# Adding p to eight row blocks by accumulating transfers, in a fused block-attention and residual LayerNorm kernel

## The chip, the cores and the metric

One core of a Trainium2 chip. The metric is the device time of one execution in microseconds; a kernel's time is the median of its runs, and one more execution is recorded by the hardware profiler.

## The reference

x has 8 batches of 512 x 1024 floats. Each batch is cut into 8 blocks of 64 rows; a block's rows are summed, the sums are projected by Wk, scored against one query vector and weighed by a softmax; their weighted sum is projected by Wo. The result, one vector p per batch, is added to every row, and a LayerNorm of that is added to x. Cut to what matters:

```python
block_repr = x.reshape(B, 8, 64, H).sum(axis=2)
keys = rms_norm(block_repr @ Wk.T) * rms_weight
attn = softmax((keys * query[1]).sum(-1))
p = ((attn[..., None] * block_repr).sum(1) @ Wo.T)[:, None, :]
z = x + p
out = x + (z - z.mean(-1)) / sqrt(z.var(-1) + 1e-6) * gamma + beta
```

## The kernel before

The 4096 rows are worked on as 32 row blocks ("rows" below) of 128 partitions x 1024 floats. Two of them make a tile of 1 MB, loaded and stored as one. Batches go in three groups of 2, 4 and 2: the first has rows 0 to 7 (tiles x0.0 to x0.3), the second rows 8 to 23 (x1.0 to x1.7), the third rows 24 to 31. Rows are gathered in units: 0 and 1 (first group), 2 to 5 of four rows each (8-11, 12-15, 16-19, 20-23), then 6 (24-27), 7 and 8 (two rows each).

For each group: `bs` (TensorE) sums the blocks of each tile as it lands; `col` (VectorE) transposes the sums; `proj.0` multiplies by Wk; `sm` is a softmax of small steps that go between VectorE, ScalarE, GpSimd and TensorE; `proj.1` multiplies by Wo; `v` weighs (vw), `p mm` spreads p over the partitions and two copies `p cp0` and `p cp1` bring its halves to SBUF (pb); `tb` writes p's rows into a small table for TensorE, by transfers.

For each row k of a group, with p there:

- `S` (VectorE, line 646) x <- x + p, with its sum over the row in tot.
- `Q` (ScalarE, line 648) squares of (sum - 1024 x), summed: the variance.
- per unit, the small steps `U.. v` (variance with epsilon), `std`, `rs` (its inverse), `s2` and `sd2` (entries of a stats matrix), mostly on GpSimd; `U.. mm` transposes that matrix on TensorE and `U.. lt` copies it to SBUF.
- `D` (VectorE, line 746) (gamma + std) * x into a pair of PSUM banks; `R` (TensorE, line 732) adds mean, beta and p as products of the stats matrix and the table; `E` (ScalarE, line 761) scales by rs and writes the result over x; `st` stores a tile (SP's queue).

Every engine works its queue in order. The queues are written out by hand in ORDER, a list of step numbers in which a word such as `72:7` gives a tile's slot (of 13) or a PSUM bank, a letter picks one of a step's engines, and `f`, `h`, `z` words are TensorE's products with zeros, which set a bank's state or fill time. The PSUM pairs 0, 2 and 4 hold the rows between D and E; a D waits until the E of the row that held its pair before is done. Loads, `tb` and stores are all issued by SP; a load into a slot that held another tile waits for that one's last reader or its store.

The kinds of a unit are set by UKIND. In the kernel before all are 'c', the path above; two other kinds are in the code and not in use.

Of the kernel before, what the change touches and what calls it, by code (L numbers as in the profile page):

```python
# [10 lines left out]
ALU = mybir.AluOpType  # L11
# [7 lines left out]
GROUPS = (2, 4, 2)  # L19
XSLOTS = 13  # L20
UNITS = ((4, 4), (4, 4, 4, 4), (4, 2, 2))
# [3 lines left out]
NTAB = 2  # L25
UKIND = 'ccccccccc'
TABS = ((0, 'y'), (1, 'y'), (2, 'y'))
# [15 lines left out]
ORDER = (  # L43
# [21 lines left out]
)  # L65
# [65 lines left out]
def block_attn_resid_kernel(  # L131
# [55 lines left out]
    def bank(name):  # L187
        return bank_at(plan.at[name])
# [25 lines left out]
    blkT = [alloc(f"blkT{i}", [P, HC, 32]) for i in range(2)]  # L214
    vw = [alloc(f"vw{i}", [P, QU]) for i in range(2)]
    pb = [alloc(f"pb{i}", [P, H]) for i in range(2)]
# [307 lines left out]
    def spread_out(G):  # L524

        n, g = G["n"], G["g"]
        name = f"proj{n}.1"
        w = vw[n % 2]
        add(f"v{n} w", [(ACT, 0.47), (DVE, 0.42)], lambda e: nc.scalar.activation(
            w, bank(name)[:, :QU], AF.Identity, scale=wcol) if e == ACT else nc.vector.tensor_scalar(  # L530
            w, bank(name)[:, :QU], wcol, None, ALU.mult), reads=["wcol"], writes=[f"vw{n % 2}"], use=name, release=name)
        part = f"p{n}"

        add(f"{part} mm", [(PE, 1.0)], lambda e: spread_p(G, part, True), reads=[f"vw{n % 2}", f"spread{g}"], claim=("P", part))
        for i in range(2):
            add(f"{part} cp{i}", [(ACT, 0.6), (DVE, 0.69)], lambda e, i=i: copy(
                e, bands(pb[n % 2])[:, :, i, :], half(part, i).rearrange("p (q d) -> p q d", d=P)),
                reads=[("slot", part)], writes=[f"pb{n % 2}.{i}"], release=part)

    def spread_p(G, part, start):  # L540
        n, g = G["n"], G["g"]
        for j in range(2):
            for i in range(2):
                lo = slice(64 * i, 64 * i + 64)
                nc.tensor.matmul(
                    half(part, i).rearrange("p (q j d) -> p j q d", j=2, d=HB)[:, j], spread[g][lo, j, :],
                    vw[n % 2][lo, :].rearrange("p (q d) -> p q d", d=HB),
                    start=start and j == 0, stop=True, tile_position=(64 * i, 0), skip_group_check=True,
                )
# [26 lines left out]
    def form_of(k):  # L576

        return "y" if kind_of(k) == "c" else "x"

# [10 lines left out]
    def before(k):  # L590

        q, r = unit_of[k]
        u = q % NU
        if kind_of(k) == "b":
            b = ubn[:, k % 2]
            add(f"B{k}", [(DVE, 1.24)], lambda e: both_halves(b, x_row(k)), reads=[xk(k)], writes=[f"ubn{k % 2}"])
            add(f"C{k}", [(DVE, 0.2)], lambda e: nc.vector.bn_aggr(out=umv[u][:, r, :], in_=b),
                reads=[f"ubn{k % 2}"], writes=[f"umv{u}.{r}"])
        elif kind_of(k) == "p":
            add(f"B{k}", [(ACT, 1.28)], lambda e: nc.scalar.activation(square, x_row(k), AF.Identity, accum_out=usx[u][:, r : r + 1]),  # L600
                reads=[xk(k)], writes=[f"usx{u}.{r}"])

    def before_p(G):
# [14 lines left out]
    def moments(k):  # L618
# [14 lines left out]
        elif kind == "p":  # L633
            y = f"y{k}"

            def go():
# [3 lines left out]
                spread_p(G, y, False)  # L640
            add(f"Y{k}", [(PE, 2.75)], lambda e: go(), reads=["ident", xk(k), f"vw{n}", f"spread{g}"], claim=("t", y))
            add(f"Q{k}", [(ACT, 1.28)], lambda e: nc.scalar.activation(
                square, flat(pair(y)), AF.Square, bias=total, scale=-float(H), accum_out=ssq),
                reads=[S], writes=[Q], use=y, release=[y, y])
        else:
            add(f"S{k}", [(DVE, 1.15)], lambda e: nc.vector.scalar_tensor_tensor(  # L646
# [4 lines left out]
    def totals(q):  # L651
# [7 lines left out]
        t = pmv[n]  # L659
        if UKIND[q] == "p":  # L660
            add(f"U{q} to", [(POOL, 0.5)], lambda e: nc.gpsimd.tensor_scalar(
# [6 lines left out]
    def unit(q):  # L668
# [5 lines left out]
        T = f"U{q}"  # L674
        st, lt = stat[i][:, :U], lts[i]
        S4 = [f"tot{i}.{r}" for r in range(U)]
# [6 lines left out]
        if UKIND[q] == "b":  # L683
# [4 lines left out]
                reads=Q4, writes=[V])  # L688
            add(f"{T} v", [(E, c)], lambda e: engine[e].tensor_tensor(v, v, a, ALU.add), reads=[f"ua{u}"], writes=[V])
        else:  # L690
            add(f"{T} v", [(E, c), (ACT, 0.25)] + ([(DVE, 0.18)] if slow else []), lambda e: nc.scalar.activation(  # L691
# [5 lines left out]
        else:  # L697
            inverse_root(T, v, r0, a, rs, (V, f"u0{u}", f"ua{u}", f"urs{u}"))
            add(f"{T} sd", [(E, c)], lambda e: engine[e].tensor_tensor(std, v, rs, ALU.mult), reads=[V, f"urs{u}"], writes=[S])
        add(f"{T} s2", [(E, c)], lambda e: engine[e].tensor_scalar(  # L700
            st[:, :, :, 0], tot[i][:, :U].unsqueeze(2).to_broadcast([P, U, 2]), -UP / H, None, ALU.mult),
            reads=S4, writes=[f"stat{i}.s"])
        D, own = f"stat{i}.d", f"stat{i}.n"
        W = 1 + MAXG if UKIND[q] == "c" else 1
        if W == 1 and (q < NST or UKIND[q - NST] == "c" or units[q - NST][0] < G["first"]):
            add(f"{T} sn", [(POOL, c + 0.1)], lambda e: nc.gpsimd.tensor_scalar(
# [197 lines left out]
```

## Time and profile before

| | us |
|---|---|
| median of three runs | 147.21 (146.16 to 147.56) |
| profiled execution | 145.84 |
| its span (first to last instruction) | 144.1 |
| VectorE busy | 98.1 (68%) |
| ScalarE busy | 89.4 (62%) |
| TensorE busy with products | 113.1 (79%) |
| GpSimd busy | 54.3 (38%) |

Busy times are from the profiled execution. A busy TensorE is not one at its peak, since its products overlap and some only fill time. Instructions that overlap by their start and end on one engine (S lasts 1.22 us, and the next begins 1.15 us after it) are counted once in a stretch's busy time.

### The profile page before, as it was taken

Reading aid. Unit: us, or ns where it says so; the run is one execution under the profiler, and the core shown is the slowest. Engines: PE = TensorE matmul, PEld = TensorE weight load, DVE = VectorE, ACT = ScalarE, POOL = GpSimd, SP = SyncE. Lnnn points to the kernel's source line nnn. Section 1 sums busy time; section 2 is a strip of 40 time slices with the busy share of each in tenths; the row PEclk is TensorE's granted clock in tenths of the full one; section 3 lists DMA queues with packets and bytes.
Section 4 is the critical chain, followed back from the end, with each engine's and each line's share of the span. In section 5 each row is a group of like instructions: output and inputs, shape, how many; then the busy total and the mean of one; then the engine's idle time right before and its main releaser. Section 6 shows DMA issues by size and latency. Waiting matters only on the chain.

```text
span 144.1 us, 2877 instructions
## 1 busy us (share of the span) xinstructions
PE 113.1 (79%) x1096; PEld 57.9 (40%) x1104; DVE 98.1 (68%) x163; ACT 89.4 (62%) x137; POOL 54.3 (38%) x108
## 2 busy tenths in 40 slices
PE   5987754989999676999673969979698798369660
PEld 2556452848985322543321224434254222123210
DVE  2056330315215996667989999999998999997920
ACT  3020210113931998065689999799979999989640
POOL 6888800000000073038001876138348009994000
PEclk9999998699999999999999599999779968999955
DMA  4999999999999997006399867644653651837894
GB/s 127 429 412 421 416 401 420 408 409 425 412 430 418 417 413 324 18 2 289 130 332 416 332 262 296 255 180 184 259 218 161 266 232 73 357 155 291 326 367 184
DMA packets 7526, 42.76 MB, mean 297 GB/s; under 512 B 808, under 2 KB 808, under 8 KB 3672
## 3 DMA queue, kind: packets, MB, share of 16 engines
q1 hardware_dynamic: 7440, 42.54, 73.0%
q8 instruction: 8, 0.13, 0.4%
q10 hardware_dynamic: 72, 0.04, 0.1%
q14 instruction: 6, 0.05, 0.1%
HBM read 25.73 MB, written 16.78 MB: 295 GB/s over the span
## 4 chain that ended last, share of the span: by engine, by line
DMA 28%; DVE 22%; PE 19%; ACT 11%; POOL 10%; issue 6%; POOLq 1%; DVEq 0%
DVE x L646 10%; DVE t L746 9%; DMA gam<-in_L_cond_ln_gamma_dram 9%; DMA x<-in_L_cond_Wo_dram 8%; PE b L473 7%; DMA x<-in_L_cond_Wk_dram 6%; POOL ustd L695 4%; ACT x L761 4%; PE t L407 4%; ACT square L648 3%; POOL urs L715 3%; DMA tab<-in_L_cond_ln_gamma_dram 3%; PE t L732 3%; DMA pb<-in_cond_dram 3%; ACT woT L241 2%
## 5 line engine op out<-in xcount | busy, mean ns | idle before, releaser
L746 DVE SCALAR_TENSOR_TENSOR t<-gam,ustd,x 128x1024 f32<-128x1024 f32 x31 | 39.0, 1290 | 5.7 <-ACT x L761 2.7
L648 ACT ACTIVATE square<-x,tot 128x1024 bf16<-128x1024 f32 x32 | 36.7, 1147 | 2.9 <-DVE x L646 2.0
L761 ACT ACTIVATE x<-t,urs 128x1024 f32<-128x1024 f32 x31 | 33.3, 1105 | 7.3 <-PE t L732 5.4
L646 DVE SCALAR_TENSOR_TENSOR x<-x,pb 128x1024 f32<-128x1024 f32 x32 | 37.4, 1216 | 0.1
L732 PE MATMUL t<-tab,lt 32*128 32x512 f32 x124 | 23.4, 652 | 3.3 <-DVE lt L243 2.1
L869 PE MATMUL b<-zeros 128*128 128x512 bf16 (+1 forms) x69 | 21.7, 452 | 3.0 <-DVE zeros L294 1.6
L407 PE MATMUL t<-ident,x 128*128 128x128 f32 x120 | 16.7, 300 | 4.3 <-DMA x<-in_L_cond_Wk_dram 2.7
L700 POOL TENSOR_SCALAR stat<-tot 128x8 f32<-128x8 f32 (+1 forms) x8 | 5.7, 714 | 36.6 <-DVE x L646 36.6
L407 PEld LDWEIGHTS t<-ident,x 128*128 128x128 f32 x120 | 15.8, 199 | 5.5 <-issue 4.8
L869 PEld LDWEIGHTS <-zeros 128*128 128x128 bf16 x90 | 9.5, 116 | 20.2 <-issue 15.9
L715 POOL TENSOR_TENSOR urs<-uv,halfs 128x4 f32<-128x4 f32 (+1 forms) x8 | 12.8, 1604 | 8.5 <-DVE uv L692 8.2
L429 PE MATMUL b<-x,blk 128*32 128x256 f32 x128 | 9.4, 416 | 5.9 <-DMA x<-in_x_dram 5.0
L241 ACT COPY wkT<-t 128x1024 f32<-128x1024 f32 x3 | 3.0, 1012 | 16.8 <-PE t L407 16.8
L732 PEld LDWEIGHTS t<-tab,lt 32*128 32x128 f32 x124 | 6.8, 186 | 14.3 <-issue 5.3
L243 DVE COPY wkT<-t 128x1024 f32<-128x1024 f32 x5 | 6.0, 1221 | 9.5 <-PE t L407 9.5
L695 POOL TENSOR_TENSOR ustd<-uv,halfs 128x4 f32<-128x4 f32 (+1 forms) x8 | 11.1, 1387 | 1.1 <-ACT uv L691 0.9
L473 PE MATMUL b<-wkT,blkT 128*32 128x256 f32 x192 | 11.0, 381 | 0.6 <-DVE blkT L439 0.6
L429 PE MATMUL t<-x,blk 128*32 128x256 f32 x128 | 8.1, 383 | 2.7 <-DMA x<-in_x_dram 2.7
L241 ACT COPY woT<-t 128x1024 f32<-128x1024 f32 x5 | 4.9, 1008 | 7.7 <-PE t L407 7.7
L486 POOL TENSOR_TENSOR ca<-c 128x8 f32<-128x8 f32 x3 | 1.6, 530 | 19.9 <-ACT c L485 19.9
L473 PE MATMUL b<-woT,blkT 128*32 128x256 f32 x128 | 7.9, 383 | 0.9 <-DVE lt L243 0.9
L473 PEld LDWEIGHTS b<-wkT,blkT 128*32 128x32 f32 x192 | 5.9, 110 | 5.8 <-DVE blkT L439 1.8
(93 smaller groups left out, 106.4 us busy)
## 6 DMA issues: line engine op xcount, KB each, us to landing
x<-in_x_dram SPq DMA_DIRECT2D x16, 1024.0 KB
out_dram<-x SPq DMA_DIRECT2D x14, 1024.0 KB
x<-in_L_cond_Wk_dram SPq DMA_DIRECT2D x4, 1024.0 KB
x<-in_L_cond_Wo_dram SPq DMA_DIRECT2D x3, 1024.0 KB
out_dram<-x SPq DMA_DIRECT2D x3, 512.0 KB
x<-in_L_cond_Wo_dram SPq DMA_DIRECT2D x2, 512.0 KB
gam<-in_L_cond_ln_gamma_dram SPq DMA_DIRECT2D x1, 512.0 KB
out_dram<-x SPq DMA_DIRECT2D x2, 256.0 KB
```

Source lines behind the costliest of these rows:

```text
L241: nc.scalar.copy(dst, src)
L407: nc.tensor.transpose(half(part, c // 4)[:, bass.ts(c % 4, P)], tile_of(name)[:, e % RT, c::HC], ident)
L429: nc.tensor.matmul(bank(f"bs{n}")[32 * j : 32 * j + 32, :QU], blk[G["g"]], tile_of(name)[:, r, bass.ts(j, QU)], start=(t == 0 and r == 0), ...
L473: nc.tensor.matmul(bank(name)[32 * j : 32 * j + 32, :QU], b[:, c, :], w[:, c, j], start=(c == 0), stop=(c == HC - 1),)
L646: add(f"S{k}", [(DVE, 1.15)], lambda e: nc.vector.scalar_tensor_tensor(x_row(k), x_row(k), 1.0, pb[n], ALU.mult, ALU.add, accum_out=total) ...
L648: add(f"Q{k}", [(ACT, 1.28)], lambda e: nc.scalar.activation(square, x_row(k), AF.Square, bias=total, scale=-float(H), accum_out=ssq), rea ...
L695: add(f"{T} std", [(POOL, 0.5 + 0.16 * U)], lambda e: nc.gpsimd.tensor_tensor(std, v, halfs[:, :1].to_broadcast([P, U]), ALU.pow), reads=[ ...
L715: add(f"{T} rs", [(POOL, 0.5 + 0.16 * U)], lambda e: nc.gpsimd.tensor_tensor(rs, v, halfs[:, 1:].to_broadcast([P, U]), ALU.pow), reads=[V, ...
L732: nc.tensor.matmul(half(f"row{k}", h), lts[q % NST][lo : lo + 32, r // RT, :], tab_of(k)[0][lo : lo + 32, :], start=False, stop=True, skip ...
L746: add(f"D{k}", [(DVE, 1.21)], lambda e: nc.vector.scalar_tensor_tensor(flat(pair(name)), gam, std, x_row(k), ALU.add, ALU.mult), reads=["g ...
L761: add(f"E{k}", [(ACT, 1.13)], lambda e: nc.scalar.activation(x_row(k), flat(pair(name)), AF.Identity, scale=rs), reads=[RS], writes=[xk(k) ...
L869: nc.tensor.matmul(bank_at(i)[:, :n], zeros, zeros[:, 0:1].to_broadcast([P, n]), start=start, stop=True, skip_group_check=True)
```

## The change

Unit 3 (rows 12 to 15) becomes kind 'a' and unit 4 (rows 16 to 19) kind 'd'. For both, S is gone; four transfers `A12`, `A14`, `A16`, `A18`, issued by GpSimd, each add pb to a tile of two rows in SBUF (read x, read p, write x).

- 'a': a step B per row sums x before p is added (`tensor_reduce` on VectorE for rows 12, 13 and 15, ScalarE for row 14); `Bp1.0` sums p (VectorE); `U3 to` (GpSimd) adds the two; Q follows as before, on the row with p.
- 'd': B is two `bn_stats` over half a row each, C is `bn_aggr`, both VectorE, on the row with p; U4's v and s2 are made from them, and there is no Q.

The slots of x go from 13 to 14, and vw from two buffers to one. ORDER is new throughout. The core of the diff:

```diff
-XSLOTS = 13
+XSLOTS = 14
-UKIND = 'ccccccccc'
+UKIND = 'cccadcccc'
...
+ADD_ISSUE = 1.3
+ADD_MB = 2.0
...
-    vw = [alloc(f"vw{i}", [P, QU]) for i in range(2)]
+    vw = [alloc("vw0", [P, QU])]
...
+        elif kind_of(k) in "pa":
+            sx = usx[u][:, r : r + 1]
+            add(f"B{k}", [(ACT, 1.34), (DVE, 1.2)], lambda e: nc.scalar.activation(
+                square, x_row(k), AF.Identity, accum_out=sx) if e == ACT else nc.vector.tensor_reduce(sx, x_row(k), AX.X, ALU.add),
                 reads=[xk(k)], writes=[f"usx{u}.{r}"])
...
+        if mine & set("bpa"):
+            add(f"Bp{n}.0", [(ACT, 1.34), (DVE, 1.2)], lambda e: nc.scalar.activation(
+                square, pb[n % 2], AF.Identity, accum_out=t[:, 0:1]) if e == ACT else nc.vector.tensor_reduce(
+                t[:, 0:1], pb[n % 2], AX.X, ALU.add),
...
+        elif kind in "ad":
+            if place[k][1] % RT == 0:
+                tile_ = x_name(k)
+                add(f"A{k}", [(POOL, ADD_ISSUE)], lambda e: nc.gpsimd.dma_start(
+                    out=tile_of(tile_), in_=pb[n].unsqueeze(1).to_broadcast([P, RT, H]), accum_op=ALU.add),
+                    reads=p_keys, writes=[xk(k), xk(k + 1)], mb=ADD_MB)
+            if kind == "a":
+                add(f"Q{k}", [(ACT, 1.34)], lambda e: nc.scalar.activation(
+                    square, x_row(k), AF.Square, bias=total, scale=-float(H), accum_out=ssq), reads=[xk(k), S], writes=[Q])
+            else:
+                b = ubn[:, k % 2]
+                add(f"B{k}", [(DVE, 1.3)], lambda e: both_halves(b, x_row(k)), reads=[xk(k)], writes=[f"ubn{k % 2}"])
+                add(f"C{k}", [(DVE, 0.2)], lambda e: nc.vector.bn_aggr(out=umv[u][:, r, :], in_=b),
+                    reads=[f"ubn{k % 2}"], writes=[f"umv{u}.{r}"])
...
+        elif UKIND[q] == "d":
+            add(f"{T} v", [(E, c), (DVE, 0.18)] if slow else [(E, c)], lambda e: engine[e].tensor_scalar(
+                v, umv[u][:, :U, 1], UP * UP, EPS * UP * UP, ALU.mult, ALU.add),
```

The queues of the second group that ORDER gives, before and after, from gamma's scaling to the third group's S24 (small softmax steps left out):

```
VectorE before: gam up, col1, D0, D1, U0 lt, D2, U1 v, sm1.., D3, sm1.., D4, sm1.., D5, U1 lt, sm1.., D6, D7, S8 to S16,
  D8, D9, D10, col2, S17, S18, D11, D12, S19, U3 lt, sm2.., D13, D14, S20, S21, D15, S22, sm2.., S23, U4 lt, D16, D17,
  sm2.., D18, sm2.., v2, D19, D20, S24
VectorE after: col1, gam up, D0, D1, D2, sm1.., D3, sm1.., D4, sm1.., D5, U1 lt, sm1.., p1 cp0, S8, S9, D6, S10, S11, D7,
  Bp1.0, D8, D9, S20, S21, D10, D11, S22, col2, S23, D12, D13, D14, B17, sm2.., B16, C16, C17, B19, C19, D15, sm2..,
  B18, C18, sm2.., U4 v, U5 lt, sm2.., v2, D16, D17, D18, S24
ScalarE before: E4, p1 cp1, p1 cp0, E5, Q8 to Q14, E6, E7, U2 lt, Q15, Q16, E8, E9, Q18, sm2.., E10, E11, Q19, Q17, E12, E13
ScalarE after: p1 cp1, E4, Q8, Q9, E5, Q10, Q11, U2 v, E6, E7, Q12, U2 lt, Q13, E8, E9, Q14, Q15, U3 v, Q22, E10, E11, Q23,
  sm2.., U3 lt, Q21, Q20, U5 v, E12, E13
GpSimd after: U1's steps, sm1.., A12, A14, A16, A18, U2 s2, U2 std, U3 to, U2 sd2, U3 s2, U2 rs, U3 std, U3 rs, U3 sd2, U5's, U4's
SP after: tb0, x2.1, st1, st3, x2.2, tb1, x2.3, st5, st7, st9, st11, st13, st15, tb2, st17
```

Ahead of this, B12, B13 and B15 stand on VectorE around the first group's v0 (B12, B13, v0, B15, p0 cp0, S0) and B14 on ScalarE ahead of p0 cp1. Two of TensorE's fills stand between the parts of the second group's first projection, ahead of D2. The second group's third pair of PSUM banks is given up: bank 0 holds the third group's block sums (`bs2`) from before p1 until col2, and rows 6 to 11 use pairs 2 and 4. On SP, x2.1 is loaded ahead of st1, x2.2 after st3, x2.3 after the second group's `tb`.

## Rows read from the trace of the kernel before

**Rows 1.** The page: busy us of each engine, share of the span, instructions.
```profile
PE 113.1 (79%) x1096; PEld 57.9 (40%) x1104; DVE 98.1 (68%) x163; ACT 89.4 (62%) x137; POOL 54.3 (38%) x108
```

**Rows 2.** Busy time by stage: from:to, length, busy us (instructions), clock, transfers' share, GB/s.
```profile
40.00:57.00 17.00, 13.90 (x257) 7.48 (x251) 11.33 (x20) 11.17 (x19) 3.86 (x5) 1.00 0.99 408
57.00:74.00 17.00, 14.53 (x177) 6.56 (x182) 12.46 (x24) 8.71 (x17) 4.38 (x4) 1.00 0.36 132
74.00:90.00 16.00, 12.17 (x124) 4.57 (x121) 16.00 (x25) 15.27 (x24) 8.59 (x9) 0.89 0.83 332
90.00:110.00 20.00, 17.45 (x168) 8.21 (x161) 19.20 (x34) 18.03 (x29) 9.45 (x14) 0.91 0.51 211
110.00:132.00 22.00, 17.29 (x74) 6.03 (x74) 21.08 (x29) 20.60 (x32) 12.18 (x11) 0.92 0.55 228
```

**Rows 3.** TensorE's timeline (start, us, what, idle before): block sums as tiles land.
```profile
49.87 1.07 PE L429 MATMUL t<-x,blk 128*32 128x256 f32 x16 [1.39 <-DMA x<-in_x_dram]
...
52.36 1.07 PE L429 MATMUL t<-x,blk 128*32 128x256 f32 x16 [0.66 <-DMA x<-in_x_dram]
...
54.85 1.07 PE L429 MATMUL t<-x,blk 128*32 128x256 f32 x16 [0.67 <-DMA x<-in_x_dram]
```

**Rows 4.** The chain that ended last (start, us, what): two transfers, and the tail.
```profile
39.20 4.45 DMA tab<-in_L_cond_ln_gamma_dram
...
43.67 12.40 DMA gam<-in_L_cond_ln_gamma_dram
...
132.23 1.25 POOLq L899
...
133.50 0.17 DVE ua L487
```

**Rows 5.** VectorE's timeline.
```profile
42.86 0.48 DVE L530 TENSOR_SCALAR vw<-t,wcol 128x256 f32<-128x256 f32 x1 [3.54 <-PE t L459]
...
45.60 1.23 DVE L646 SCALAR_TENSOR_TENSOR x<-x,pb 128x1024 f32<-128x1024 f32 x1
...
56.10 0.69 DVE L352 TENSOR_SCALAR gam<-gam 128x1024 f32<-128x1024 f32 x1 [1.25 <-DMA gam<-in_L_cond_ln_gamma_dram]
...
75.05 1.22 DVE L646 SCALAR_TENSOR_TENSOR x<-x,pb 128x1024 f32<-128x1024 f32 x1
...
76.20 1.22 DVE L646 SCALAR_TENSOR_TENSOR x<-x,pb 128x1024 f32<-128x1024 f32 x1
...
84.22 3.68 DVE L746 SCALAR_TENSOR_TENSOR t<-gam,ustd,x 128x1024 f32<-128x1024 f32 x3
87.81 0.44 DVE L439 STREAM_TRANSPOSE blkT<-b 128x256 f32<-128x256 f32 x1
...
111.56 1.22 DVE L646 SCALAR_TENSOR_TENSOR x<-x,pb 128x1024 f32<-128x1024 f32 x1
```

**Rows 6.** ScalarE's timeline.
```profile
44.79 0.59 ACT L241 COPY pb<-b 128x512 f32<-128x512 f32 x1 [4.05 <-PE b L545]
...
75.17 1.15 ACT L648 ACTIVATE square<-x,tot 128x1024 bf16<-128x1024 f32 x1 [0.50 <-DVE x L646]
...
76.44 1.15 ACT L648 ACTIVATE square<-x,tot 128x1024 bf16<-128x1024 f32 x1
...
88.63 2.10 ACT L761 ACTIVATE x<-t,urs 128x1024 f32<-128x1024 f32 x2
```

**Rows 7.** VectorE's copies in the list of groups: busy us, mean ns.
```profile
L243 DVE COPY lt<-b 128x256 f32<-128x256 f32 x3 | 1.3, 417 | 0.0
...
L243 DVE COPY pb<-b 128x512 f32<-128x512 f32 x1 | 0.7, 692 | 1.5 <-PE b L545 1.5
```

**Rows 8.** GpSimd's timeline.
```profile
54.94 0.25 POOL L700 TENSOR_SCALAR stat<-tot 128x8 f32<-128x8 f32 x1
...
78.73 1.08 POOL L700 TENSOR_SCALAR stat<-tot 128x8 f32<-128x8 f32 x1 [10.85 <-DVE x L646]
...
80.99 1.91 POOL L715 TENSOR_TENSOR urs<-uv,halfs 128x4 f32<-128x4 f32 x1
```

More of the change, by code (lines that the diff above doesn't have):

```diff
@@ L527, in spread_out @@
         name = f"proj{n}.1"
-        w = vw[n % 2]
+        w = vw[0]
         add(f"v{n} w", [(ACT, 0.47), (DVE, 0.42)], lambda e: nc.scalar.activation(
             w, bank(name)[:, :QU], AF.Identity, scale=wcol) if e == ACT else nc.vector.tensor_scalar(
-            w, bank(name)[:, :QU], wcol, None, ALU.mult), reads=["wcol"], writes=[f"vw{n % 2}"], use=name, release=name)
+            w, bank(name)[:, :QU], wcol, None, ALU.mult), reads=["wcol"], writes=["vw0"], use=name, release=name)
         part = f"p{n}"
-        add(f"{part} mm", [(PE, 1.0)], lambda e: spread_p(G, part, True), reads=[f"vw{n % 2}", f"spread{g}"], claim=("P", part))
+        add(f"{part} mm", [(PE, 1.0)], lambda e: spread_p(G, part, True), reads=["vw0", f"spread{g}"], claim=("P", part))
         for i in range(2):
@@ L546, in spread_p @@
                     half(part, i).rearrange("p (q j d) -> p j q d", j=2, d=HB)[:, j], spread[g][lo, j, :],
-                    vw[n % 2][lo, :].rearrange("p (q d) -> p q d", d=HB),
+                    vw[0][lo, :].rearrange("p (q d) -> p q d", d=HB),
                     start=start and j == 0, stop=True, tile_position=(64 * i, 0), skip_group_check=True,
@@ L576, in form_of @@
     def form_of(k):
-        return "y" if kind_of(k) == "c" else "x"
+        return "y" if kind_of(k) in "cad" else "x"
     def tab_of(k):
@@ L598, in before @@
                 reads=[f"ubn{k % 2}"], writes=[f"umv{u}.{r}"])
-        elif kind_of(k) == "p":
-            add(f"B{k}", [(ACT, 1.28)], lambda e: nc.scalar.activation(square, x_row(k), AF.Identity, accum_out=usx[u][:, r : r + 1]),
+        elif kind_of(k) in "pa":
+            sx = usx[u][:, r : r + 1]
+            add(f"B{k}", [(ACT, 1.34), (DVE, 1.2)], lambda e: nc.scalar.activation(
+                square, x_row(k), AF.Identity, accum_out=sx) if e == ACT else nc.vector.tensor_reduce(sx, x_row(k), AX.X, ALU.add),
                 reads=[xk(k)], writes=[f"usx{u}.{r}"])
@@ L607, in before_p @@
         mine = {UKIND[q] for q, (first, _) in enumerate(units) if G["first"] <= first < G["first"] + G["rows"]}
-        if mine & set("bp"):
-            add(f"Bp{n}.0", [(ACT, 1.28)], lambda e: nc.scalar.activation(square, pb[n % 2], AF.Identity, accum_out=t[:, 0:1]),
+        if mine & set("bpa"):
+            add(f"Bp{n}.0", [(ACT, 1.34), (DVE, 1.2)], lambda e: nc.scalar.activation(
+                square, pb[n % 2], AF.Identity, accum_out=t[:, 0:1]) if e == ACT else nc.vector.tensor_reduce(
+                t[:, 0:1], pb[n % 2], AX.X, ALU.add),
                 reads=[f"pb{n % 2}.{i}" for i in range(2)], writes=[f"pmv{n % 2}.0"])
@@ L640, in go @@
                 spread_p(G, y, False)
-            add(f"Y{k}", [(PE, 2.75)], lambda e: go(), reads=["ident", xk(k), f"vw{n}", f"spread{g}"], claim=("t", y))
+            add(f"Y{k}", [(PE, 2.75)], lambda e: go(), reads=["ident", xk(k), "vw0", f"spread{g}"], claim=("t", y))
             add(f"Q{k}", [(ACT, 1.28)], lambda e: nc.scalar.activation(
@@ L659, in totals @@
         t = pmv[n]
-        if UKIND[q] == "p":
+        if UKIND[q] in "pa":
             add(f"U{q} to", [(POOL, 0.5)], lambda e: nc.gpsimd.tensor_scalar(
@@ L674, in unit @@
         T = f"U{q}"
-        st, lt = stat[i][:, :U], lts[i]
+        st, lt, dst = stat[i][:, :U], lts[i], tot[i][:, :U]
         S4 = [f"tot{i}.{r}" for r in range(U)]
@@ L689, in unit @@
             add(f"{T} v", [(E, c)], lambda e: engine[e].tensor_tensor(v, v, a, ALU.add), reads=[f"ua{u}"], writes=[V])
+        elif UKIND[q] == "d":
+            add(f"{T} v", [(E, c), (DVE, 0.18)] if slow else [(E, c)], lambda e: engine[e].tensor_scalar(
+                v, umv[u][:, :U, 1], UP * UP, EPS * UP * UP, ALU.mult, ALU.add),
+                reads=[f"umv{u}.{r}" for r in range(U)], writes=[V])
         else:
@@ L699, in unit @@
             add(f"{T} sd", [(E, c)], lambda e: engine[e].tensor_tensor(std, v, rs, ALU.mult), reads=[V, f"urs{u}"], writes=[S])
+        mean = (umv[u][:, :U, 0], 1.0) if UKIND[q] == "d" else (dst, 1.0 / H)
         add(f"{T} s2", [(E, c)], lambda e: engine[e].tensor_scalar(
-            st[:, :, :, 0], tot[i][:, :U].unsqueeze(2).to_broadcast([P, U, 2]), -UP / H, None, ALU.mult),
-            reads=S4, writes=[f"stat{i}.s"])
+            st[:, :, :, 0], mean[0].unsqueeze(2).to_broadcast([P, U, 2]), -UP * mean[1], None, ALU.mult),
+            reads=[f"umv{u}.{r}" for r in range(U)] if UKIND[q] == "d" else S4, writes=[f"stat{i}.s"])
         D, own = f"stat{i}.d", f"stat{i}.n"
-        W = 1 + MAXG if UKIND[q] == "c" else 1
-        if W == 1 and (q < NST or UKIND[q - NST] == "c" or units[q - NST][0] < G["first"]):
+        W = 1 + MAXG if UKIND[q] in "cad" else 1
+        if W == 1 and (q < NST or UKIND[q - NST] in "cad" or units[q - NST][0] < G["first"]):
             add(f"{T} sn", [(POOL, c + 0.1)], lambda e: nc.gpsimd.tensor_scalar(
```

43 rows, old and new, of the table ORDER are left out of this document.

## The prediction

> **What bounds the kernel now.** I began with the page's busy shares [rows 1]: no engine fills the span, so I cut the span by stages [rows 2]. To 57 us the transfer engines are full (408 GB/s) and everything waits for loads. From 57 to 74 nothing is full: a chain of small steps (projection, softmax, projection, p of the second group) crosses all engines. From 74 to 132 VectorE is busy 56.28 of 58 us, ScalarE 53.90, transfers little over half from 90 on. Then comes a tail. So VectorE's queue sets the pace from 74 to 132, with ScalarE close behind, and taking work from VectorE there can pay in full only where it doesn't meet the chain of 57 to 74, a wait for a PSUM pair, or the tail, which the chain of waits leads through GpSimd and unit 8's small steps, as its last two rows here show [rows 4].
>
> **Prices.** A row of S occupies VectorE 1.15 us from start to start, a row of D 1.20 (three D's lie between 84.22 and 87.81) [rows 5]. A row of Q occupies ScalarE 1.27 us, an E 1.0 [rows 6]. The copy of a stats bank (lt) is 0.42 us, some 0.34 from start to start, and half of p 0.69, some 0.6 [rows 7].
>
> **Taken from VectorE after 57 us.** S12 to S19: 8 x 1.15 = 9.2. Three copies lt that go to ScalarE on balance: 1.0. Together 10.2.
>
> **Given to VectorE after 57 us.** B16 to B19, two statistics passes over 512 elements each: the trace has none. Bounds: one S (1.15 us, the same elements in one instruction) and two copies of 512 (1.38) [rows 5, 7]; I take 1.25, as two fixed costs lie between, so 5.0. C16 to C19 are small steps like those at the tail, 0.2 each: 0.8. Bp1.0, a sum over 1024 elements: 1.15, as an S. The half of p that ScalarE copied: 0.6. Two small v steps: 0.3. Together 7.85. VectorE gains 2.3 us (1.8 to 2.7), ScalarE 4 x 1.27 + 0.6 - 1.0 = 4.7.
>
> **The sums of x ahead of p** (B12 to B15) run before 57 us, where VectorE waited 3.54 us for the first group's projection and ScalarE 4.05 [rows 5, 6]. They aren't free: they sit ahead of the step v0 in VectorE's queue. Tiles of x land 2.49 us apart, the sixth, seventh and eighth at 49.87, 52.36 and 54.85 [rows 3]; counting back, x1.2 lands at 42.4 and x1.3 at 44.9. B12 and B13 (1.15 each) then hold v0 from 42.86 to 44.7, and S0 begins near 47.0 instead of 45.60. Cover: VectorE waited 1.25 us at 56.10 for gamma [rows 5]. S7 now ends at 56.1 and D0 begins at 57.15 against 57.08. Cost nothing; without gamma's wait it would be 1.4.
>
> **57 to 74.** New fills between the projection's parts let D2 start earlier, unit 1's v on GpSimd comes before the softmax step, and p1's halves are copied side by side. Following the new queues with the rows' durations, S8 starts at about 72.2 instead of 73.91. But D6 and D7 (2.4 us) are now behind S8, where before they were done: 0.7 us lost.
>
> **The new wait at D8.** The transposed block sums of group 2 now hold bank 0 until col2, so D6 to D11 alternate between pairs 2 and 4. D8 needs E6, which needs R6, which needs D7. D7 ends at 79.2; R6 1.14 and E6 1.05 bring 81.5, and unit 2's std on GpSimd (after Q11 at 79.9 and v, 1.1 to 1.9 us [rows 8]) 81.3 to 82.2. Only Bp1.0 (to 80.35) lies between: VectorE idles some 1.7 us. Behind D8 in the queue are all rows that remain. Before, nine S ran there without a wait.
>
> **The sum with adds that cost no wait.** By the same walk S24 begins at 109.7 with D19 and D20 still to do (2.4): the work stands at 112.1 where before it stood at 111.56 [rows 5]. In the tail unit 8's chain reaches its step n2 at 133.95 against 133.50 [rows 4]. So +0.4 us: the 2.3 that VectorE saves goes into D6 and D7 (0.7), the wait at D8 (1.7) and smaller waits at D12 and D16.
>
> **The adds.** Four transfers of 1 MB, A12 to A18, issued by GpSimd once p1 is in SBUF (72.2). GpSimd idled 10.85 us before 78.73 [rows 8], so four issues fit if each takes up to 2 us; no row shows one. Bounds: 0.25 us (its shortest steps) and 1.91 us [rows 8]; I take 1.2. Behind them on GpSimd are U2's steps. Small GpSimd steps take 0.25 us while VectorE idles (54.94) and 1.08 beside S rows (78.73) [rows 8]. "SBUF — State Buffer" in the Trainium skill, Who interferes with whom, says that a VectorE instruction with two SBUF inputs holds up only GpSimd work that reads SBUF; it takes the writing of descriptors to need the other interface, so by that page the issues are not stretched, and by the rows read alone each might be, by 0.8 us.
>
> How long does an add take? A plain load of 1 MB takes 2.49 us of the full transfer engines [rows 3]. That is the lower end: an add writes 1 MB too. It reads 2 MB (p and x) where a plain transfer reads one: 5.0 if reading sets the pace; with reading and writing in turn, three passes, 7.5. I take 4.4: nearer to two passes than to either end. And they share: a 2 KB transfer that ScalarE issued at 39.20 landed 4.45 us later, while gamma, issued on SP's queue at 43.67 behind the loads, needed 12.40 [rows 4]; so another engine's queue isn't put behind all of SP's, both get turns. "DMA: Bandwidth & Descriptors" in the Trainium skill, SWDGE vs HWDGE vs iDMA, says the same, an engine going round its queues, and it would put a further 2 us of completion on each landing (an estimate from its section on one DMA's anatomy); by that the price below would be some 2 us higher.
>
> Now the landings, with half the rate while SP's queue has work: SP has x2.3 (issued 74.5), st5 (77.3), st7 (82.5), st9 (87.8), each 5 us at half rate, so without a gap until 94.5. A12 starts at 73.7 and lands at 81.7; Q12 is due at 82.5: in time. A14 lands at 90.5; Q14 is due at 87.8: ScalarE stands 2.7 us, and behind Q14 are Q15, U3's v and E10, so VectorE stands as long at D12. A16 lands at 96.9, in time for B17 (now due at 98.5). A18 meets st11 and lands at 103.7; B19 is due at 101.8: VectorE stands 1.9. Together 4.6 us. With 3.7 us an add it is 1.7; with 5.0 it is 7.1; with 2.49 nothing.
>
> **How the sum stands to the times.** 145.84 + 0.4 + 4.6 = 150.8. The profiled execution (span 144.1, 1.74 around it) lies 1.4 under the median of runs, 147.21, so I forecast 152.2. Changes under 1% (1.5 us) can't be told from none: the three runs of before span 1.4.
>
> **Rivals.** (a) *The adds are cheap or early enough.* If an add takes under 3.7 us at half rate, or SP's stores yield to them, A14 lands before Q14 is due and only the +0.4 is left: 146.2, as a median 147.6. For it: transfers are only half used after 90 [rows 2], and stores have nobody waiting for them. Against it: from 74.5 to 94.5 stores and x2.3 leave no gap beside four adds, whose engine time is 17.6 us.
>
> (b) *The saving arrives, faster.* One mechanism: adds under 3.7 us as in (a), and at D8 the queues close up, because E6 and U2's std come sooner than I walk them (S8 at 71 instead of 72.2 does it, as D6 and D7 then lie in time that was idle before). Then VectorE's 2.3 us count in full: 143.5, median 144.9. For it: VectorE's share of 97% from 74 to 132. Against it: D8's wait comes from the order of D7, R6 and E6 themselves, which move together with S8.
>
> (c) *The adds take three passes.* 7.5 us each: A14 lands near 101, A18 near 120: 20 us lost, 167. Nothing in the trace speaks for it but nothing excludes it.
>
> (d) *GpSimd's issues are the wait.* At 4 us each they end at 88 instead of 78, and U2's std, then D8, come 6 to 8 us late, of which the adds' own lateness covers part: 154. For it: the stretched steps [rows 8]; against: 0.25-us steps when it is free.
>
> **How the numbers follow.** Forecast (late adds) 0.47, rival (d) 0.04, (c) 0.04, (a) 0.25, (b) 0.20. The likeliest one's own range, from 3.7 to 5.5 us an add, is 148.8 to 156.5. The range that holds 8 in 10 must take in (a) and most of (b): 144.4 to 156.5. It leaves out (c), half of (d) and the ends of both. Faster by over 1%: 0.20. Within 1%: (a), with a little of the forecast's lower end and of (b): 0.26. Slower: 0.54.
>
> **What the profile will show.** Right: waits of ScalarE at Q14 and of VectorE at B19 that end with a transfer on GpSimd's queue; VectorE idle 1 to 2 us ahead of D8 on E6; S8 near 72; S0 near 47; D0 near 57.1; transfers full from 74 to about 100. B in the 1.15 to 1.38 bounds. Wrong: no wait on a transfer at Q12, Q14, B17 and B19, each add landing within 10 us of its issue, which makes it (a) or (b); a gap before U2's std on GpSimd with the issues ahead of it, which makes it (d). The forecast is also wrong if stores simply come later and the adds go first, for then col2, waiting for x2.3, shows the wait instead.

## The result and the profile after

The changed kernel takes 161.32 us (160.54 to 162.59), before 147.38 in the same runs: a ratio of 1.097, interval 1.087 to 1.107. Slower, as forecast, but by 13.9 us where 5 were forecast, and outside the range. The profiled execution took 161.58, its span is 159.9: 15.8 longer than before's 144.1.

First the page: busy shares, granted clock and transfer share in 40 slices of 4.0 us, then the two queues that matter.

```profile
PE 119.6 (75%) x1097; PEld 57.0 (36%) x1097; DVE 100.0 (63%) x164; ACT 86.9 (54%) x135; POOL 54.9 (34%) x108
...
PEclk9999999999999999999759569999569999587965
DMA  4999999999999980569999999999141665426594
...
q1 hardware_dynamic: 7440, 42.54, 65.7%
q0 software_dynamic: 1088, 4.19, 13.7%
...
x<-pb POOLq DMA_DIRECT2D x4, 1024.0 KB, 25.2
```

q0 is the adds' queue: 4.19 MB in 13.7% of 159.9 us, that is 21.9 us of all 16 engines, 5.5 us an add. Issue to landing took 25.2 us at the median.

The stages, to be held against [rows 2]:

```profile
57.00:74.00 17.00, 16.16 (x204) 7.18 (x203) 11.48 (x21) 9.55 (x18) 5.35 (x8) 1.00 0.54 200
74.00:90.00 16.00, 8.23 (x42) 2.75 (x44) 10.45 (x14) 10.78 (x17) 8.62 (x10) 0.73 1.04 286
90.00:110.00 20.00, 16.77 (x183) 6.96 (x181) 13.69 (x22) 15.23 (x25) 7.16 (x8) 0.88 1.03 289
```

The third busy column is VectorE's. From 74 to 110 it idled 11.9 of 36 us; before, 0.8. In the same stretch the transfer engines went from 0.83 and 0.51 to full, and yet moved only 286 to 289 GB/s (plain loads: 408, [rows 2]). Full engines at a low rate mean that something slow is on them.

Where VectorE stood, in its timeline (compare [rows 5]; the brackets give the idle time and what ended it):

```profile
47.16 1.23 DVE L667 SCALAR_TENSOR_TENSOR x<-x,pb 128x1024 f32<-128x1024 f32 x1
...
57.54 1.29 DVE L772 SCALAR_TENSOR_TENSOR t<-gam,ustd,x 128x1024 f32<-128x1024 f32 x1
...
73.10 1.23 DVE L667 SCALAR_TENSOR_TENSOR x<-x,pb 128x1024 f32<-128x1024 f32 x1
...
85.48 2.49 DVE L772 SCALAR_TENSOR_TENSOR t<-gam,ustd,x 128x1024 f32<-128x1024 f32 x2 [4.19 <-issue]
89.33 1.23 DVE L667 SCALAR_TENSOR_TENSOR x<-x,pb 128x1024 f32<-128x1024 f32 x1 [1.36 <-issue]
...
92.92 2.49 DVE L772 SCALAR_TENSOR_TENSOR t<-gam,ustd,x 128x1024 f32<-128x1024 f32 x2 [1.02 <-ACT x L787]
97.70 1.23 DVE L667 SCALAR_TENSOR_TENSOR x<-x,pb 128x1024 f32<-128x1024 f32 x1 [2.29 <-ACT square L659]
...
101.31 3.69 DVE L772 SCALAR_TENSOR_TENSOR t<-gam,ustd,x 128x1024 f32<-128x1024 f32 x3 [0.89 <-POOL ustd L720]
104.91 1.28 DVE L591 BATCH_NORM_STATS2 ubn<-x 128x6 f32<-128x512 f32 x2
...
110.82 1.29 DVE L591 BATCH_NORM_STATS2 ubn<-x 128x6 f32<-128x512 f32 x2 [2.79 <-DMA x<-pb]
...
122.05 1.22 DVE L667 SCALAR_TENSOR_TENSOR x<-x,pb 128x1024 f32<-128x1024 f32 x1
...
147.78 1.29 DVE L772 SCALAR_TENSOR_TENSOR t<-gam,ustd,x 128x1024 f32<-128x1024 f32 x1 [3.00 <-ACT x L787]
```

These are S0, D0, S8; D8 (4.19 idle), S20, D10, S22, D12, B17, B19 (2.79), S24 and D29 (3.00). S24 stands at 122.05 with D19 and D20 still to do (2.4 us), so the work is 12.9 us behind before's 111.56; D29's wait of 3.0 gives the rest of the 15.8.

ScalarE's timeline says whom S20 and S22 waited for (Q12 and Q14, compare [rows 6]):

```profile
84.27 2.12 ACT L787 ACTIVATE x<-t,urs 128x1024 f32<-128x1024 f32 x2 [3.52 <-PE t L758]
87.99 1.15 ACT L659 ACTIVATE square<-x,tot 128x1024 bf16<-128x1024 f32 x1 [1.60 <-DMA x<-pb]
...
96.43 1.15 ACT L659 ACTIVATE square<-x,tot 128x1024 bf16<-128x1024 f32 x1 [2.53 <-DMA x<-pb]
```

Q12, Q14 and B19 wait for A12, A14 and A18, which land at 87.9, 96.3 and 110.7. S20 to S23 (unit 5) wait for the Q of unit 3, because these two units share one buffer of totals (tot, by the unit's number mod 2): S20 may overwrite what Q12 reads only once Q12 is done. E8 and U3's std (D10, D12) stand behind Q13 and Q15.

D8's wait leads to TensorE:

```profile
78.86 1.94 PE L432 MATMUL t<-x,blk 128*32 128x256 f32 x16 [4.10 <-DMA x<-in_x_dram]
80.73 1.46 PE L895 MATMUL b<-zeros 128*128 128x512 bf16 x3
82.12 2.09 PE L758 MATMUL t<-tab,lt 32*128 32x512 f32 x8
```

The first row is bs2.2, the block sums of tile x2.2, which the new order puts ahead of R6. TensorE stood 4.1 us for that tile. When the eight products of R6 and R7 (third row) at last ran the granted clock was 0.50, that is 1.2 GHz, and they took 2.09 us where eight such products at 2.4 GHz took 1.14. Then E6 at 84.27, then D8.

### The profile page after: what moved, and what is told of

The parts are those of the page before. It is cut to its first block, busy times and chain, and to the rows that moved or that the text cites. A ratio compares the mean times of both kernels' runs of the same rounds, so it can differ in the third digit from the quotient of the medians.

```text
span 159.9 us, 2871 instructions
## 1 busy us (share of the span) xinstructions
PE 119.6 (75%) x1097; PEld 57.0 (36%) x1097; DVE 100.0 (63%) x164; ACT 86.9 (54%) x135; POOL 54.9 (34%) x108
## 3 DMA queue, kind: packets, MB, share of 16 engines
q0 software_dynamic: 1088, 4.19, 13.7%
## 5 line engine op out<-in xcount | busy, mean ns | idle before, releaser
L772 DVE SCALAR_TENSOR_TENSOR t<-gam,ustd,x 128x1024 f32<-128x1024 f32 x31 | 39.0, 1288 | 11.9 <-ACT x L787 5.8
L758 PE MATMUL t<-tab,lt 32*128 32x512 f32 x124 | 28.0, 754 | 11.0 <-DVE t L772 6.7
L667 DVE SCALAR_TENSOR_TENSOR x<-x,pb 128x1024 f32<-128x1024 f32 x24 | 28.5, 1225 | 3.9 <-ACT square L659 2.3
L669 ACT ACTIVATE square<-x,tot 128x1024 bf16<-128x1024 f32 x24 | 27.5, 1148 | 2.4 <-DVE x L667 1.5
L895 PE MATMUL b<-zeros 128*128 128x512 bf16 x73 | 25.3, 487 | 3.1 <-DVE zeros L297 2.1
L432 PE MATMUL t<-x,blk 128*32 128x256 f32 x192 | 13.1, 408 | 7.4 <-DMA x<-in_x_dram 6.6
L410 PE MATMUL t<-ident,x 128*128 128x128 f32 x120 | 14.9, 278 | 4.8 <-DMA x<-in_L_cond_Wk_dram 2.8
L410 PEld LDWEIGHTS t<-ident,x 128*128 128x128 f32 x120 | 14.0, 191 | 6.6 <-issue 4.3
L246 DVE COPY wkT<-t 128x1024 f32<-128x1024 f32 x4 | 4.8, 1223 | 10.6 <-PE t L410 10.6
L432 PEld LDWEIGHTS t<-x,blk 128*32 128x32 f32 x192 | 5.7, 115 | 13.8 <-DMA x<-in_x_dram 8.3
L655 POOL DMA_DIRECT2D x<-pb x4 | 5.1, 2006 | 6.9 <-ACT pb L244 6.9
## 6 DMA issues: line engine op xcount, KB each, us to landing
x<-pb POOLq DMA_DIRECT2D x4, 1024.0 KB, 25.2
x<-in_L_cond_Wo_dram SPq DMA_DIRECT2D x3, 1024.0 KB, 13.2
```

What stands on the lines that cost most here:

```text
L410: nc.tensor.transpose(half(part, c // 4)[:, bass.ts(c % 4, P)], tile_of(name)[:, e % RT, c::HC], ident)
L432: nc.tensor.matmul(bank(f"bs{n}")[32 * j : 32 * j + 32, :QU], blk[G["g"]], tile_of(name)[:, r, bass.ts(j, QU)], start=(t == 0 and r == 0), ...
L669: add(f"Q{k}", [(ACT, 1.28)], lambda e: nc.scalar.activation(square, x_row(k), AF.Square, bias=total, scale=-float(H), accum_out=ssq), rea ...
L758: nc.tensor.matmul(half(f"row{k}", h), lts[q % NST][lo : lo + 32, r // RT, :], tab_of(k)[0][lo : lo + 32, :], start=False, stop=True, skip ...
L772: add(f"D{k}", [(DVE, 1.21)], lambda e: nc.vector.scalar_tensor_tensor(flat(pair(name)), gam, std, x_row(k), ALU.add, ALU.mult), reads=["g ...
L895: nc.tensor.matmul(bank_at(i)[:, :n], zeros, zeros[:, 0:1].to_broadcast([P, n]), start=start, stop=True, skip_group_check=True)
```

## The experiments

Three theories. **1**: four adds need some 5 us each of all transfer engines; their late landings set the pace. **2**: the new order's own waits (D8, the tail) are the loss, whatever the adds cost. **3**: the four issues on GpSimd are the loss. All ratios are to before, in the same runs.

**Adds of 32 columns** (p stays out of the other 992 columns of rows 12 to 19). All steps, waits and issues remain.

```diff
-out=tile_of(tile_), in_=pb[n].unsqueeze(1).to_broadcast([P, RT, H]), accum_op=ALU.add),
+out=tile_of(tile_)[:, :, :32], in_=pb[n][:, :32].unsqueeze(1).to_broadcast([P, RT, 32]), accum_op=ALU.add),
```

> The changed kernel with adds that touch 32 of the 1024 columns of each row (the rest of rows 12 to 19 stays without p): order, issues and waits stay, the transfer time is gone. Theory 1 (four adds need some 5 us each of all transfer engines, and their late landings set the pace): the last statistics pass starts near 99 instead of 110.8, 147 to 150 us. Theory 2 (the new order's own waits cost most: two PSUM pairs, shared totals of units 3 and 5, the tail): 155 or more. Theory 3 (the issues on GpSimd are the wait): 158 or more, since all four issues are still there.

Measured 149.37, ratio 1.015 (1.008 to 1.023). So about 12.0 of the 13.9 us go away with the adds' transfers (161.32 less 149.37), and about 2 stay with the order. Theory 3 falls, since all four issues are still there. Of the 12.0, 9.9 are gained up to S24 (112.18 against 122.05) and the rest in the tail, where D29's wait of 3.0 us is gone too; the tail has an experiment of its own below. Of VectorE's waits above, only D8's is left:

```profile
85.56 2.49 DVE L772 SCALAR_TENSOR_TENSOR t<-gam,ustd,x 128x1024 f32<-128x1024 f32 x2 [3.97 <-issue]
...
112.18 1.22 DVE L667 SCALAR_TENSOR_TENSOR x<-x,pb 128x1024 f32<-128x1024 f32 x1
```

And in TensorE's, bs2.2 begins at the same time as with whole adds, so they don't delay that load:

```profile
79.01 1.93 PE L432 MATMUL t<-x,blk 128*32 128x256 f32 x16 [3.96 <-DMA x<-in_x_dram]
```

**Plain copies for adds** (p is written over x; x is lost in those rows).

```diff
-..., in_=pb[n].unsqueeze(1).to_broadcast([P, RT, H]), accum_op=ALU.add),
+..., in_=pb[n].unsqueeze(1).to_broadcast([P, RT, H])),
```

> The changed kernel with plain copies of p over x in place of the adds (x is lost in rows 12 to 19): same queue, same issues, same bytes written, but no reading of x and no adding. Theory 1 with two passes for an add: a copy costs 2.5 us of the engines, four cost 10 us less than four adds, the last lands near 98 and the time is 148 to 152. If a copy issued by GpSimd is as slow as an add, the price is not in the adding, and the time stays at 159 or more. Theories 2 and 3: 158 or more.

151.23, ratio 1.029 (1.021 to 1.037). From the queue table:

```profile
q0 software_dynamic: 1088, 4.19, 7.2%
```

7.2% of 149.3 us: 2.7 us a copy, half of an add, and no step waits for one. The same packets and bytes at half the engine time save 10.1 us.

**One transfer by itself**, in the kernel before: p of the first group onto tile x2.0 while the transfer engines are idle (the third group then works on an x with that p added, or on that p instead of x), once as an add, once as a copy.

```diff
+    add("X", [(POOL, 1.3)], lambda e: nc.gpsimd.dma_start(
+        out=tile_of("x2.0"), in_=pb[0].unsqueeze(1).to_broadcast([P, RT, H]), accum_op=ALU.add),
+        reads=["pb0.0", "pb0.1"], writes=["x2.0.0", "x2.0.1"])
```

> The kernel before with one more transfer: p of the first group added to tile x2.0 (1 MB) once that is loaded, near 58.5, when the transfer engines stand still until 65 (the third group's results are spoilt). This shows an add alone: 5.0 us of full engines if it costs two passes of a load (2.49), 2.5 if one, 7.5 if three. Time of the kernel: 146 to 148, as nothing waits for it.

> The same with a plain copy of p over tile x2.0 in place of the add: 2.5 us of full engines if GpSimd's queue moves bytes as SP's does. The difference to the run with one add is what reading x and adding cost. Time of the kernel: 146 to 148.

Each was run once, for its trace. Windows of 1 us, the last two columns transfer share and GB/s; first the add:

```profile
60.00:61.00 1.00, 1.00 (x24) 0.59 (x20) 0.00 (x0) 0.00 (x0) 0.57 (x1) 1.00 0.00 0
61.00:62.00 1.00, 1.00 (x14) 0.23 (x7) 0.00 (x1) 0.45 (x2) 0.00 (x0) 1.00 1.02 188
...
65.00:66.00 1.00, 1.00 (x24) 0.48 (x16) 0.65 (x2) 0.54 (x3) 1.00 (x1) 1.00 1.07 188
```

then the copy:

```profile
62.00:63.00 1.00, 1.00 (x12) 0.24 (x16) 1.00 (x1) 0.00 (x0) 0.00 (x0) 1.00 1.00 373
63.00:64.00 1.00, 1.00 (x17) 0.42 (x17) 0.83 (x5) 0.91 (x1) 0.59 (x1) 1.00 0.51 188
```

An add fills all engines at 188 GB/s, for 5.9 us (4.1% of its span of 144.4). A copy runs at 373 and needs 2.9 (2.0% of 146.4). Both were issued at 59.15; from issue to landing the add took 8.3 us, the copy 5.8. Of these, 2.0 and 1.5 us passed before the first packet moved (the add's row from 60 to 61 is empty), and 0.3 and 0.4 us between the last packet and the landing. The issue occupied GpSimd for 1.42 and 0.95 us.

**Which adds cost.** First unit 4's two (A16, A18) cut to 32 columns, then unit 3's two (A12, A14) instead: the same bytes.

```diff
+                cols = H if kind == "a" else 32
...
-                    out=tile_of(tile_), in_=pb[n].unsqueeze(1).to_broadcast([P, RT, H]), accum_op=ALU.add),
+                    out=tile_of(tile_)[:, :, :cols], in_=pb[n][:, :cols].unsqueeze(1).to_broadcast([P, RT, cols]), accum_op=ALU.add),
```

> The adds of unit 3 whole, those of unit 4 cut to 32 columns. Theory 1: the first two adds land as before (88 and 96), the waits ahead of S20 and S22 stay, and only the wait of B19 (2.8 us) and what later stores shared with the adds fall away: 157 to 159. Theory 2: no change, 160 to 162. If the whole price belongs to the last landing (110.8), it falls to about 150.

> The other half of the run with two adds: those of unit 3 cut to 32 columns, those of unit 4 whole. The bytes that the transfer engines add are the same, but the rows are read first by B17, near 96 to 100, not by Q12 and Q14, near 82 to 88. If an add's price is its landing against the time its row is due (theory 1), the second lands near 96 and the time is 149 to 151. If it is the engines' time as such, or GpSimd's part, the time is that of the two adds of unit 3: 158 to 160.

With A12 and A14 whole 159.14, ratio 1.079 (1.073 to 1.085); with A16 and A18 whole 152.45, ratio 1.038 (1.031 to 1.044). The first is at the upper edge of what theory 1 expected, the second 1.5 us above it. Over the 149.37 with none, the early pair costs 9.8, the late pair 3.1, both together 12.0. The early pair's rows show the same waits as after, at Q14 for instance:

```profile
97.00 1.15 ACT L660 ACTIVATE square<-x,tot 128x1024 bf16<-128x1024 f32 x1 [3.36 <-DMA x<-pb]
```

With the late pair no step waits for an add, and S24 begins at 112.97, 0.8 later than with none; with the early pair it begins at 120.22, 8.0 later. So the same bytes cost 8.0 us up to S24 where the rows are due early and 0.8 where they are due late: not the bytes are the price, but the landing against the due time. The rest of both pairs' price falls in the tail. With the early pair D29 stood 3.26 us, as in after. With the late pair TensorE's granted clock was 0.57 and 0.50 from 122 to 134; with adds of 32 columns it was 0.62 only from 122 to 126, then 1.00. What these two parts have to do with the adds isn't shown.

**bs2.2 behind R6**, in the changed kernel.

```diff
 ORDER, TensorE's part:
-... fill, bs2.2, (fill), R6, ...
+... fill, (fill), R6, bs2.2, ...
```

> One step moved: the block sums of tile x2.2 stand behind R6 on TensorE and not ahead of it, so the late load of x2.2 (78.86) no longer holds R6, E6 and D8. VectorE's wait of 4.2 us ahead of D8 shrinks to 1.5. Theory 1: S20 still waits for Q12 and Q12 for the first add (88), so the total falls by 0 to 1 us: 160 to 161.5. If TensorE's queue is what delays (theory 2), the total falls by 2.5 to 4 us: 157.5 to 159.

159.08, ratio 1.077 (1.071 to 1.084), 2.2 us less: more than theory 1 expected, and at the edge of theory 2's range. But VectorE's timeline shows that the gain was not where the edit is:

```profile
82.25 1.33 DVE L771 SCALAR_TENSOR_TENSOR t<-gam,ustd,x 128x1024 f32<-128x1024 f32 x1 [0.61 <-POOL ustd L719]
...
88.92 1.23 DVE L666 SCALAR_TENSOR_TENSOR x<-x,pb 128x1024 f32<-128x1024 f32 x1 [3.75 <-ACT square L658]
...
110.72 1.29 DVE L590 BATCH_NORM_STATS2 ubn<-x 128x6 f32<-128x512 f32 x2 [2.80 <-DMA x<-pb]
```

D8 runs 3.2 us earlier, S20 then waits 2.4 us more for Q12 (3.75 for 1.36), and B19 is where it was. S24 begins 0.3 us earlier (121.73); the rest of the 2.2 us came from the tail, where U7's rs lasted 1.19 us instead of 2.32 and the 3-us wait at D29 is absent. With whole adds D8's wait cost next to nothing: the wait for A12 came behind it.

**The tail.** In after, GpSimd runs U7's rs ahead of sd2, for which TensorE waits:

```profile
139.22 2.32 POOL L741 TENSOR_TENSOR urs<-uv,halfs 128x2 f32<-128x2 f32 x1
141.51 1.13 POOL L736 TENSOR_TENSOR stat<-ustd,ind 128x20 f32<-128x20 f32 x1
```

The experiment swaps the two.

```diff
 ORDER, GpSimd's part:
-... U7 std, U7 rs, U7 sd2 ...
+... U7 std, U7 sd2, U7 rs ...
```

> The changed kernel with one step moved: unit 7's rs stands behind its sd2 on GpSimd, as in the kernel before. In the tail of the changed kernel rs took 2.32 us ahead of sd2, TensorE stood still 2.6 us for it and ran on at the lower clock, and D29 came 3.0 us late. If that is where the last 2 to 3 us went, the time falls to 158 to 159.5. If the tail is set by something else, it stays at 160.5 to 162.5.

159.40, ratio 1.082 (1.074 to 1.091): 1.9 less, D29's wait gone, B19's wait still 2.79.

**The order by itself, and both together.** 32-column adds with bs2.2 behind R6; then with both edits; then whole adds with both edits.

> Small adds (32 columns) and the block sums of x2.2 behind R6: the changed order without the adds' transfer time and without that wait of TensorE. If the 2.2 us by which small adds are slower than the kernel before are the wait of D8 for the load of x2.2, the time is that of before, 146.5 to 147.7, with D8 near 82 instead of 85.56. If the order costs by its pairs, totals and tail, 149 or more stays.

> Small adds, the block sums of x2.2 behind R6, unit 7's rs behind sd2: the changed order without its two stalls and without the adds' transfer time, the best that adds that cost nothing could give here. The two stalls are worth 1.8 us (S24 in the runs with small adds) and some 2.5 us (tail): 146.5 to 148, level with the kernel before. If VectorE's saved 2.3 us came through, 144.5 to 145.5.

> The same two moves with whole adds. Theory 1: S20 and S22 still wait for Q12 and Q14, B19 for the last add near 110.7, so the time is 8 to 11 us above the run with small adds and the same moves: 156 to 158.5. If the stalls of the order were what the adds' price came from, the two would lie within 4 us.

150.95, ratio 1.024 (1.018 to 1.029); 149.07, 1.011 (1.006 to 1.016); 159.16, 1.083 (1.077 to 1.090). With both waits of the order away, the adds cost 10.1 us. So of the 13.9 us some 10 belong to the adds, some 2 to the tail's wait (which the swap alone took away) and some 2 to the rest of the order. All three times lie above what was expected. The first is even above the 149.37 of 32-column adds alone: in its profile S8 begins 1.2 us later (74.62), U7's rs lasts 2.32 us again, and D29 stands 3.25. With 32-column adds the edits that I expected to bring the kernel level with before bring nothing that lasts. With both, S24 begins at 110.29, 1.9 earlier than with neither, and the last D at 136.87 against 136.88. The gain is lost in the tail. First TensorE's windows with 32-column adds and the order as changed, then with both edits (the third number from the end is the granted clock):

```profile
130.00:134.00 4.00, 2.76 (x15) 1.20 (x16) 3.20 (x7) 3.31 (x6) 1.19 (x2) 1.00 0.31 125
```

```profile
130.00:134.00 4.00, 4.00 (x14) 1.06 (x13) 2.26 (x4) 2.06 (x5) 0.00 (x0) 0.50 0.41 168
```

At 0.50 (1.2 GHz) U7's fills and first R's took 1.91 and 2.09 us instead of 1.03 and 1.40:

```profile
129.36 0.48 PE L746 MATMUL b<-ident,stat 128*128 128x128 f32 x1 [1.28 <-POOL stat L735]
129.62 1.91 PE L894 MATMUL b<-zeros 128*128 128x512 bf16 x4
131.47 2.09 PE L757 MATMUL t<-tab,lt 32*128 32x512 f32 x8
```

In both kernels TensorE had stood 1.3 us for U7's stats matrix before them, so that wait alone doesn't decide the clock. Why it fell in one and not in the other stays open.

**Another place for an add.** Before's order, with unit 5 alone as kind 'a': its sums of x on ScalarE and VectorE between 56 and 61, A20 issued at 84.68 and A22 at 91.70.

```diff
-UKIND = 'cccadcccc'
+UKIND = 'cccccaccc'
 ORDER: that of before; S20 to S23 out, B20 to B23 between 56 and 61 us, Bp1.0 behind S16, A20 and A22 behind two of U3's steps
```

> A version for use: the order of the kernel before, with the added rows only in unit 5 (rows 20 to 23, kind a): two adds and not four, issued after the loads of the third group (A20 near 86, A22 near 91) and due near 100 and 104; sums of x by ScalarE and VectorE where they stood idle near 58. VectorE loses 4 x 1.15 and gains 1.15 for the sum of p. Theory 1: two adds of 5.6 us against stores at half the engines land near 96 and 106, so Q22 may wait 1 to 2 us; ScalarE is nearly as full as VectorE, so at most 1 to 1.5 us can come through: 145.5 to 148.

150.64, ratio 1.021 (1.014 to 1.028). The expectation failed. Landing took 14.0 us at the median (two adds, stores beside them), and ScalarE stood again:

```profile
107.54 1.15 ACT L658 ACTIVATE square<-x,tot 128x1024 bf16<-128x1024 f32 x1 [3.39 <-DMA x<-pb]
```

Behind this Q22 stood small softmax steps of the third group, and VectorE waited 3.58 us for them. No version beats before.

## Why the prediction was off

**Direction and mechanism held.** Adds and SP's stores take turns, the adds land late, ScalarE stands at Q14 and VectorE at B19. S0 47.16 (47.0 forecast), D0 57.54 (57.15), S8 73.10 (72.2), transfers full from 74 to 110; a B takes 1.28 (1.25 taken, within its bounds), Bp1.0 1.21 (1.15). The adds had 21.9 of the 37.1 us from first issue to last landing, 59%: the half share was nearly right.

**The step that failed is the landing of the adds.** A12 landed at 87.9 instead of 81.7, A14 at 96.3 instead of 90.5, A18 at 110.7 instead of 103.7. Four terms make up A12's 6.2 us.

*The size*: 4.4 us taken, 5.5 measured (5.9 for the one by itself), 2.2 plain loads of 2.49 [rows 3]. The price for two reads, 5.0, was closer than the value that I took. At half share this is 2.2 us.

*The start*: I let A12 transfer from 73.7. It was issued at 73.61, and its first packet moved at 75.8: 2.1 us. The Trainium skill, "DMA: Bandwidth & Descriptors", Anatomy of one DMA, gives about 2 us a transfer for setup and completion, which the prediction named and left out of its sum. The trace agrees with the size and not with the place: the page puts most of it behind the last byte, but the add by itself waited 2.0 us ahead of its first packet and 0.3 behind its last.

*The neighbours* gave some 2 us back. I shared the engines from 74.5 on. But from 76 to 80 the transfer engines were full at 193 GB/s, close to the 188 of an add alone, so the adds had them nearly to themselves; the sharing began at 80:

```profile
72.00:76.00 4.00, 2.76 (x18) 0.82 (x14) 3.60 (x6) 3.11 (x5) 2.39 (x3) 1.00 0.97 332
76.00:80.00 4.00, 1.14 (x12) 0.59 (x16) 4.00 (x6) 3.97 (x6) 3.61 (x4) 0.73 1.10 193
80.00:84.00 4.00, 4.00 (x19) 0.80 (x11) 1.29 (x2) 0.72 (x3) 3.01 (x6) 0.50 0.98 286
```

*The last packets*: no term of mine, and the largest, 3.5 us. In the trace of the packets each add ends with 16 packets of 4 bytes, as many as there are transfer engines. Fifteen of A12's come between 83.4 and 84.1, the sixteenth at 87.6, and 0.3 us behind it A12 lands. I read this as one engine that runs behind the others. A14's sixteenth comes 2.2 us behind its fifteenth, A16's 1.7, A18's 1.4; for the add by itself all sixteen lie within 0.4 us. The load of x2.2 shows the same gap (2.2 us, up to 78.5). Why one runs behind stays open.

The spacing of the landings came out close to the walk, 8.4 us to A14 (8.8 forecast) and 14.4 to A18 (13.2), but that is luck in part: 5.5 us an add at half share would have been 11.

**The place of the wait failed too.** I let VectorE stand at D12, behind Q14. It stood at S20, D10, S22 and D12, 5.6 us together instead of 2.7, since unit 5's S waits for unit 3's Q through the shared totals: four S's that I had run without a wait hung on the same transfers.

**The wait at D8 was mis-sized**: 4.19 against 1.7. I had R6 wait for D7, and missed bs2.2 ahead of R6. R6 doesn't need D7: with bs2.2 behind it, it ran right behind D6, and D8 stood only 0.61 us, for U2's std:

```profile
77.08 1.13 PE L757 MATMUL t<-tab,lt 32*128 32x512 f32 x4 [1.33 <-DVE t L771]
```

A row of before, which I hadn't read, has such a load landing as late:

```profile
79.01 1.93 PE L429 MATMUL b<-x,blk 128*32 128x256 f32 x16 [2.19 <-DMA x<-in_x_dram]
```

There too a tile of the third group, issued at 70.63, lands at 79.0; behind bs then stood nothing that VectorE needed. But this term is not the loss: with whole adds it lies under the wait for A12, as moving bs2.2 showed.

**The order cost 2.2 us**, not 0.4, by the 32-column adds. There S24 begins at 112.18, where the walk without waits for adds had 109.7; 2.3 of these 2.5 us are D8's wait (3.97 against 1.7). With the two visible waits away S24 begins at 110.29, near the walk, and yet 1.6 us are left by the ratio (1.011). They are lost in the tail, beside TensorE's lower clock; that the clock is the cause isn't shown.

**The tail** I put at almost nothing. In after D29 stood 3.0 us in it, behind U7's rs and sd2 on GpSimd, and the swap of the two gave 1.9 back. VectorE's S24 was forecast at 109.7 + 4.6 = 114.3 and begins at 122.05: of these 7.8 us, 0.9 stem from S8's start, 2.5 more than forecast stand at D8, 2.9 at S20 to D12, 0.9 at B19, and 0.6 in smaller waits.

**The rivals.** (a), adds early, and (b), the saving arrives: both need adds under 3.7 us at half rate, and no add is. (c), three passes of 7.5 us: excluded by 5.5 to 5.9; the time came nearer to it than to the forecast all the same, because the landings were late by more than the size. (d), GpSimd's issues: four took 5.14 us, done at 78.7, and U2's std (80.83) waited for U2's v and not for them. "SBUF — State Buffer" in the Trainium skill, Who interferes with whom, had them not stretched beside VectorE; 1.28 us each beside S rows against 1.42 for a single one agrees.

**The range** ended at 156.5 because the walk of the forecast was ended with 5.5 us an add. That is the measured size; what the walk leaves out even so is the late start, the late last packets, the longer wait at D8 and the tail. Its lower end is a slip: 145.84 + 0.4 + 1.7 + 1.4 is 149.3, not 148.8.

## What to carry to other kernels

Before work is moved from an engine to transfers, add up the transfer engines' own time in the stretch: here 22 us of adds and some 15 of loads and stores in 37 us, with the first result due 9 us after its issue. An accumulating transfer cost 2.2 loads of its size here, not one; 2 us passed before it moved, and it had landed only with its last packets, up to 3.5 us behind the others. And follow from each late landing what shares a buffer or stands in the same in-order queue: a wait taken away ahead of a later one buys next to nothing, as D8's did.

## What the runs showed of the hardware beyond that

Accumulating into SBUF halves the rate of all 16 transfer engines, 188 GB/s against 373 for the same packets as a copy, and costs GpSimd 1.24 to 1.42 us an issue against 0.95 for the copy alone. The same small GpSimd step (U7's rs) lasted 1.19 us in one run and 2.32 in another of nearly the same program. TensorE's granted clock in the tail was 1.00 or 0.50 over the same products, in programs that differ by two moved steps or by the columns of two adds, and the tail was about 2 us longer where it was 0.50.
